# A two-layer graph network on one core: 288 counted chunks for 264, matrices of 512 and 448 columns, fewer row buffers

## The chip, the core and the metric

One core of a Trainium2 chip runs the whole program. The metric is the device time of one execution in microseconds; the figure given for a kernel is the median of its runs. The engines are named as the profile names them: PE is TensorE (PEld its weight loads), DVE is VectorE, ACT is ScalarE, POOL is GpSimd and SP is SyncE.

## What is computed

There are 6250 nodes of 256 values and 100000 edges, sorted by destination, with random sources. The destination density falls along the node numbers: edge e of E ends at about node 6250 (e/E)^2, so the early nodes have many edges each.

```
x = layernorm(x + L0(x));  x = layernorm(x + L1(x))
L0: summed = segment_sum(x[src], dst);  agg = summed / max(deg_in, 1)
    out = concat(x, agg) @ weight;  return out / norm(out) + bias
L1: h = x * rsqrt(deg_out);  m = segment_sum(h[src], dst) * rsqrt(deg_in)
    y = m @ W_gc + b_gc + x @ W_res + b_res
    y = y + top2_of_64_experts(y)          # gelu feed-forward, 256-512-256
    return batchnorm(y) * gamma + beta
```

## The kernel before

Both layers need a sum over edges, `segment_sum`. The kernel cuts the edges into NCH = 782 chunks of 128 and treats them in two ways, with the same split in both layers.

The first DCH = 264 chunks are *counted*. `counts` (L724 to L760) makes of each chunk two one-hot matrices, of its sources (`low_rows`, L705) and of source block and destination within a window of ten nodes (`oha`, L737), and multiplies them on PE (L756, 490 columns) to numbers of edges. When a group of chunks with one window ends, DVE adds the window's first column (L745) and ACT copies the other nine (L747) into an adjacency matrix kept in the on-chip memory: `adj_a` for nodes 0 to DENSE = 448 (ACH = 200 chunks), `adj_b` for nodes EDGE = 384 to EDGE + MORE = 752 (64 chunks). The matrices are later applied to all node rows by `dense_product` (L412 to L440): for each of NT = 49 node tiles of 128, six matmuls (L424) of three bf16 parts by two halves of the columns, for each matrix. A `Track` hands them out in halves of a tile, three matmuls a half. Layer 1 (the first one, L0 above) applies `adj_a` and `adj_b` one after the other, layer 2 both together. Each product is as wide as its matrix.

The other NG = 518 chunks are *gathered*: POOL issues an indirect DMA that fetches the 128 source rows (`gather_rows`, L387) into one of `nbuf` row buffers, and PE multiplies them, three bf16 parts of 256 columns, by a one-hot matrix of destinations (L664 in layer 1, L1175 in layer 2; the one-hots come from DVE four chunks at a time, `near4`, L409). Groups of chunks (GGRP) share one accumulator; at the end of a group ACT copies it (`sums`, L611 and L1179), PE transposes it (L394) and DVE adds it to `acc` (L401). Layer 1 has 9 row buffers (and for the first 64 chunks 7 others, in float32), layer 2 has 12.

One loop step is one gathered chunk, and all else is laid over these steps. `Track` spreads a list of pieces evenly between a first and a last step; `Steps` calls a piece some steps later; `staged` runs a generator in which `yield n` is a pause of n steps. PE, DVE, ACT and SP execute exactly in the order in which the loop emits (`manual_schedule`), so a piece that is late on one of these engines holds up all behind it; the same holds for DMAs on SP's queue. In layer 1:

- steps 0 to X_END = 44: the rows of x are split into three bf16 parts and stored (`three`, tiles of pool `wx3`), the matrices are cleared
- step 53 to A_END = 262: the 200 chunks of `adj_a` are counted; x times the own half of the weight (`own`, L697) is stored; `sources` counts the sources of the gathered chunks (matmuls of 49 columns, L721), until END
- A_END to END = 320: the 64 chunks of `adj_b` are counted; the dense product of `adj_a` begins and lasts to DA_END = 386
- END to DA_END: the matrices are summed to in-degrees, piece by piece of 128 nodes (`by_destination`, L785, 49 matmuls of one column at L794 for each of 7 pieces, then an add for each piece to `deg`)
- DA_END + 3 to DB_END = 476: dense product of `adj_b`
- from END + 2: every B_GAP = 3.8 steps a node tile whose sums are complete starts `first_layer` (`layer1`, L496 to L558: loads of `xw` and `xb` on SP, the product with the weight L509, norms on DVE and ACT, stores). The first ND = 6 node tiles wait for the dense products, the other 43 go first.

In layer 2 the dense products take steps 2 to D2_END = 116 (their node rows come over SP in tiles `x3`); after that `layer2` (L1043 onwards) starts a tile every T_GAP = (gathered - 128)/49 = 7.96 steps: residual (L1066) and graph product (L1070), top 2 of the experts' logits, ranks, and a table of tokens (L1203). Every 40 steps SP also issues a fill of 1792 KB with zeros. Routing, the experts' loop and the final normalization come after and share no code with the change.

`acc`, the two matrices, the constants, the one-hots and all buffers share the on-chip memory. At the start `acc` is cleared by ACT, which copies a tile `nothing` of zeros piece by piece (L269); `rel` holds each edge's place relative to its group's base, for all chunks.

Of the kernel before, what the change touches and what calls it, by code (L numbers as in the profile page):

```python
# [9 lines left out]
F32 = mybir.dt.float32  # L10
F16 = mybir.dt.float16
BF16 = mybir.dt.bfloat16
# [20 lines left out]

ACH, DCH = 200, 264
DENSE, EDGE, MORE = 448, 384, 368
ND = (EDGE + MORE + P - 1) // P
# [13 lines left out]
DX = D + NEXP  # L50
LAYER = {"xw": 3, "xb": 3, "po": 2, "o": 5, "rv": 2, "h3": 2}

# [88 lines left out]
def gnn_moe_kernel(  # L141
# [78 lines left out]
    with ExitStack() as gctx:  # L220
# [27 lines left out]

        rel = ep.tile([P, NCH], F32, name="rel")
        ngp = (NG + OHB - 1) // OHB * OHB  # L250
# [8 lines left out]
        extra = ep.tile([1, 2], I32, name="extra")  # L259
        nothing = ep1.tile([P, 512], F32, name="nothing")  # L260
        nc.vector.memset(nothing, 0.0)
# [4 lines left out]
        for h in range(2):  # L266
            for i in range(0, NACC, 512):
                n = min(512, NACC - i)
                nc.scalar.copy(acc[:, h, i : i + n], nothing[:, :n])  # L269
        with tc.tile_pool(name="pl", bufs=1) as pl, tc.tile_pool(name="pps", bufs=1, space=PSUM) as pps:  # L270
# [49 lines left out]
            bases(of_gathered)  # L320
            nc.vector.tensor_sub(rel[:, DCH:], dst_f[:, DCH:], base[:, DCH:])
            group_bases(of_gathered)
# [11 lines left out]
            nc.vector.memset(near[:, NG:], OUTSIDE)  # L334
            nc.vector.tensor_copy(near[:, :NG], rel[:, DCH:])

# [18 lines left out]
            nc.vector.tensor_scalar(out_w[:, :DCH], rel[:, :DCH], float(DWIN), None, op0=OP.is_ge)  # L355
            nc.vector.tensor_scalar(out_w[:, DCH:], rel[:, DCH:], float(P), None, op0=OP.is_ge)
            nc.vector.scalar_tensor_tensor(out_w, rel, 0.0, out_w, op0=OP.is_lt, op1=OP.add)
            real = pl.tile([P, 1], F32, name="real")
# [137 lines left out]
        def layer1(wk, ps, row, agg, rdeg, rsq_out, free, used=None):  # L496
# [24 lines left out]
            ss, sd = sm[:, 0:1], sm[:, 1:2]  # L521
            junk = wk.tile([P, D], F32, name="junk", bufs=2)
            nc.scalar.activation(junk, o, AF.Square, accum_out=ss)
# [47 lines left out]
        with ExitStack() as c:  # L571
            wk = c.enter_context(tc.tile_pool(name="wkg", bufs=2))
            ps1 = c.enter_context(tc.tile_pool(name="ps1", bufs=1, space=PSUM))
            ps2 = c.enter_context(tc.tile_pool(name="ps2", bufs=2, space=PSUM))
            nbuf, xgrp = 9, 0
            while GGRP[xgrp][0] - DCH < FIRST:
                xgrp += 1
            xch = GGRP[xgrp][0]
            bufs = []
            rsq_out = wk.tile([P, NT], F32, name="rsq_out", bufs=1)  # L580
# [124 lines left out]
            def low_rows(ohc, c0):  # L705
                ohl = ohc.tile([P, P, OHB], BF16, name="ohl")
                nc.vector.tensor_tensor(ohl, iota_lo, lo[:, None, c0 : c0 + OHB].to_broadcast([P, P, OHB]),
                                        op=OP.is_equal)
                return ohl

            def high_rows(pool, c0):
                ohh = pool.tile([P, NT, OHB], BF16, name="ohh")
                nc.vector.tensor_tensor(ohh, iota_hi, hi[:, None, c0 : c0 + OHB].to_broadcast([P, NT, OHB]),
                                        op=OP.is_equal)
                return ohh
# [8 lines left out]
            def counts(ohc, psa):  # L724
                where = {}
                for j, (c0, g) in enumerate(DGRP):
                    for ch in range(c0, c0 + g):
                        where[ch] = (j, ch == c0, ch == c0 + g - 1)
                lows, places, pa = {}, {}, [None]

                def prepare(ch):
                    if ch >= DCH:
                        return
                    if ch % OHB == 0:
                        lows[ch] = low_rows(ohc, ch), high_rows(ohc, ch)
                    oha = ohc.tile([P, NT * DWIN], BF16, name="oha", bufs=4)
                    nc.vector.tensor_scalar(oha, iota_h, rel[:, ch : ch + 1], None, op0=OP.is_equal)  # L737
                    places[ch] = oha

                def add(j, pa):  # L740

                    adj, most = (adj_a, DENSE - DWIN) if j < len(AGRP) else (adj_b, MORE - DWIN)
                    b = nc.vector.value_load(base_i[0:1, j : j + 1], min_val=0, max_val=most)
                    a = adj[:, :, ds(b, 1)]
                    nc.vector.tensor_add(a, a, pa[:, :, 0:1])  # L745
                    b = nc.scalar.value_load(base_i[0:1, j : j + 1], min_val=0, max_val=most)
                    nc.scalar.copy(adj[:, :, ds(b + 1, DWIN - 1)], pa[:, :, 1:])  # L747

                def one(ch):
                    for k in range(0, 3) if ch == 0 else (2,):  # L750
                        prepare(ch + k)
                    j, first, last = where[ch]
                    if first:
                        pa[0] = psa[0].tile([P, NT, DWIN], F32, name="pa")
                    low, high = (v[:, :, ch % OHB] for v in lows[ch - ch % OHB])
                    nc.tensor.matmul(pa[0].rearrange("p t w -> p (t w)"), low, places.pop(ch), start=first, stop=last)  # L756
                    by_source(low, high)
                    if last:
                        steps.after(2, lambda pa=pa[0]: add(j, pa))

                return [lambda ch=ch: one(ch) for ch in range(DCH)]


            def sources():
                made = {}

                def prepare(c0):
                    if c0 < NCH:
                        ohh = high_rows(ohp, c0)
                        ohs = ohp.tile([P, P, OHB], BF16, name="ohs")  # L770
                        nc.vector.tensor_tensor(ohs, iota_lo, lo[:, None, c0 : c0 + OHB].to_broadcast([P, P, OHB]),
                                                op=OP.is_equal)
                        made[c0] = ohs, ohh

                def one(c0):
                    for k in (0, 1) if c0 == DCH else (1,):
                        prepare(c0 + k * OHB)
                    ohs, ohh = made.pop(c0)
                    for k in range(min(OHB, NCH - c0)):
                        by_source(ohs[:, :, k], ohh[:, :, k])  # L780

                return [lambda c0=c0: one(c0) for c0 in range(DCH, NCH, OHB)]


            def by_destination(psg):  # L785

                pieces = [(adj_a, d, min(P, DENSE - d), d // P) for d in range(0, DENSE, P)]
                pieces += [(adj_b, d - EDGE, min(P, EDGE + MORE - d), d // P) for d in range(EDGE, EDGE + MORE, P)]
                pg = psg.tile([P, len(pieces)], F32, name="pg")

# [6 lines left out]
                def add():  # L797
                    for w, (_, _, n, t) in enumerate(pieces):
                        a = deg[:n, t : t + 1]
                        nc.vector.tensor_add(a, a, pg[:n, w : w + 1])  # L800

# [29 lines left out]

            X_END, A_END, END = 44, 262, 320
            DA_END, DB_END, B_GAP = 386, 476, 3.8
            with tc.manual_schedule(engines=ordered), ExitStack() as c1:
                cx, ca, cb, hold, cd, cg = (ExitStack() for _ in range(6))
                wx3 = cx.enter_context(tc.tile_pool(name="wx3", bufs=7))
                rows_of_g = gathered()
# [9 lines left out]
                def dense(end, adj, n, to):  # L847
                    psd = cd.enter_context(tc.tile_pool(name="psd", bufs=1, space=PSUM, side="right"))
                    xd = cd.enter_context(tc.tile_pool(name="xd", bufs=4, side="right"))

# [8 lines left out]
                def work(i):  # L859
                    nonlocal due, wl, psl, ohp, dense_done  # L860
                    if i == X_END + 9:
# [10 lines left out]
                        psa[0] = ca.enter_context(tc.tile_pool(name="psa", bufs=3, space=PSUM))  # L872
                        wx = ca.enter_context(tc.tile_pool(name="wx", bufs=3))
                        every = counts(ohc, psa)
# [20 lines left out]
                    if i == DA_END + 3:  # L895
                        dense_done = DENSE // P
                        cd.close()
# [251 lines left out]
        with ExitStack() as c:  # L1149
            st = c.enter_context(tc.tile_pool(name="st2", bufs=1))  # L1150
            ohg = c.enter_context(tc.tile_pool(name="ohg2", bufs=4))
            wk = c.enter_context(tc.tile_pool(name="wkg2", bufs=2))
            ps1 = c.enter_context(tc.tile_pool(name="ps3", bufs=1, space=PSUM))
            both_po = ps1.tile([P, 2, 2, P], F32, name="both_po")
            nbuf, ng2 = 12, NCH - DCH
            bufs = [st.tile([P, 2, 3, P], BF16, name=f"rows3{i}") for i in range(nbuf)]
# [28 lines left out]
            def parts3(t):  # L1185
                x3 = wk.tile([P, 2, 3, P], BF16, name="x3", bufs=5)
                nc.sync.dma_start(x3, h3_rows[t * P : (t + 1) * P])
                return x3
# [492 lines left out]
```

## Time and profile before

| | before |
|---|---|
| median of 3 runs | 2268.14 us (2264.69 to 2269.84) |
| the profiled execution | 2249.79 us |
| its span | 2248.0 us |
| mean granted PE clock | 0.886 |
| layer 1, first to last gather | 7.7 to 797.9 us |
| layer 2, first to last gather | 833.2 to 1596.8 us |
| DMA | 454.74 MB, mean 202 GB/s |

The profile is that of one execution. Its page gives busy time and instruction count of each engine and the costliest groups of instructions with their mean time in ns and the idle time ahead of them, with what ended it. The view of waits sums, by engine and line, what an engine stood still for, how often, and the longest one in us. In the table of windows each row is a stretch of the span. "remote" is a release that the view cannot assign to one instruction. The layers' stages in span time follow from the starts of the gathers of steps 53, 262, 320, 389 and 479 (86, 401, 495, 604 and 743 us) and of step 116 of layer 2 (1004 us).

### The profile page before, as it was taken

The page shows a single profiled execution, that of the slowest core. Times are in us where ns is not written, and L with a number is a line of the kernel's source. Part 1 is how long each engine was busy: PE and PEld are TensorE (multiplying, and loading weights), DVE is VectorE, ACT ScalarE, POOL GpSimd, SP SyncE. Part 2 cuts the span into 40 slices and gives each one's busy share as a digit, 9 for nine tenths or more (in the row PEclk, how much of TensorE's full clock was granted, in tenths as well). Part 3 has the DMA queues.
Part 4 walks back from the last instruction along what each step waited for, and adds up shares of the span by engine and source line. Part 5 has one row for each costly group of instructions (what it writes and reads, how often), then busy time and mean ns, then how long its engine had stood idle before and what let it go on. Part 6 is the DMA issues. An engine that isn't in the chain of part 4 may idle for free. (4 is left out here: it accounts for less than half of the span.)

```text
span 2248.0 us, 33489 instructions
## 1 busy us (share of the span) xinstructions
PE 1721.7 (77%) x9410; PEld 1233.8 (55%) x9410; DVE 1056.5 (47%) x4020; ACT 589.9 (26%) x1569; POOL 1248.4 (56%) x1440
## 2 busy tenths in 40 slices
PE   4677777788888638986767766666759998999697
PEld 2355555556656425654544444444438876877573
DVE  7655666675767541102434443344532233222398
ACT  7411123343444430000211211112212221222135
POOL 7766666656656626666666666666225544454100
PEclk8798898999989868997887987888869999999899
DMA  7756666557899746775666555555348988787353
GB/s 228 267 170 177 173 176 173 169 164 244 265 301 310 237 150 203 228 226 181 190 180 176 170 158 152 151 154 155 89 144 307 322 291 266 249 257 246 106 168 114
DMA packets 245283, 454.74 MB, mean 202 GB/s; under 512 B 36462, under 2 KB 166247, under 8 KB 245086
## 3 DMA queue, kind: packets, MB, share of 16 engines
q0 software_dynamic: 74880, 220.59, 33.8%
q1 hardware_dynamic: 167886, 230.37, 31.2%
q10 hardware_dynamic: 2320, 1.51, 0.2%
q8 instruction: 80, 1.31, 0.2%
q14 instruction: 117, 0.96, 0.1%
HBM read 386.64 MB, written 70.89 MB: 204 GB/s over the span
## 5 line engine op out<-in xcount | busy, mean ns | idle before, releaser
L387 POOL DMA_INDIRECT rows<-h_rows,src_i x518 | 497.7, 961 | 266.8 <-issue 111.5
L387 POOL DMA_INDIRECT rows<-x_rows,src_i x454 | 451.2, 994 | 247.1 <-issue 91.2
L1175 PE MATMUL both_po<-rows,oh 128*128 128x256 bf16 x1554 | 256.0, 302 | 148.9 <-ACT sums L1179 72.5
L1175 PEld LDWEIGHTS <-oh 128*128 128x128 bf16 x1554 | 180.4, 120 | 207.0 <-issue 171.8
L664 PE MATMUL po<-rows,oh 128*128 128x256 bf16 (+1 forms) x1362 | 241.3, 292 | 16.0 <-issue 12.8
L1444 POOL DMA_INDIRECT core<-ob,ix x100 | 101.4, 1014 | 204.0 <-DVE ob L1443 195.5
L1442 PE MATMUL po<-w2t,h 128*128 128x256 f32 x800 | 190.8, 388 | 1.1 <-ACT h L1435 0.5
L401 DVE TENSOR_TENSOR acc<-acc,pt 128x256 f32 x108 | 45.3, 419 | 294.5 <-remote 80.6
L1435 ACT ACTIVATE h<-ph,b1c 128x128 f32<-128x128 f32 (+1 forms) x288 | 94.3, 410 | 340.2 <-PE ph L1433 160.1
L664 PEld LDWEIGHTS <-oh 128*128 128x128 bf16 x1362 | 148.4, 120 | 60.6 <-issue 27.3
L1442 PEld LDWEIGHTS po<-w2t,h 128*128 128x128 f32 x800 | 151.0, 193 | 39.9 <-ACT h L1435 18.4
L409 DVE TENSOR_TENSOR oh<-iota_lo,near 128x512 bf16<-128x512 bf16 x244 | 101.6, 423 | 111.1 <-PE both_po L1175 81.8
L1443 DVE TENSOR_TENSOR ob<-po,b2b 128x256 f32<-128x256 f32 x100 | 42.4, 424 | 228.6 <-PE po L1442 207.7
L756 PE MATMUL pa<-oha,ohl 128*128 128x490 bf16 x264 | 105.7, 400 | 48.7 <-issue 24.2
L737 DVE TENSOR_SCALAR oha<-iota_h,rel 128x490 bf16<-128x490 f16 x264 | 94.1, 363 | 58.1 <-PE pa L756 23.2
L1421 PE MATMUL ph<-xt,w1t 128*128 128x256 f32 x448 | 118.8, 406 | 0.0
L1401 POOL DMA_INDIRECT xb<-xx_tok,ix x100 | 98.4, 984 | 27.0 <-issue 25.7
L1421 PEld LDWEIGHTS ph<-xt,w1t 128*128 128x128 f32 x448 | 110.4, 326 | 5.3 <-issue 2.6
L424 PE MATMUL pd<-adj_a,x 128*128 128x448 bf16 x294 | 106.1, 365 | 5.4 <-issue 5.3
L1083 DVE TENSOR_TENSOR xl<-xl,pR 128x320 f32<-128x320 f32 x49 | 23.8, 486 | 178.1 <-issue 87.5
L1066 PE MATMUL pR<-wres,t 128*128 128x320 f32 x196 | 77.1, 524 | 29.3 <-issue 18.5
L424 PE MATMUL pd<-adj_b,x 128*128 128x368 bf16 x294 | 96.6, 329 | 1.2 <-issue 0.9
(335 smaller groups left out, 3345.0 us busy)
## 6 DMA issues: line engine op xcount, KB each, us to landing
w1t<-in_L_gnn_w_dram SPq DMA_DIRECT2D x72, 512.0 KB
w2t<-in_L_gnn_w_dram SPq DMA_DIRECT2D x72, 512.0 KB
x3d<-x_rows SPq DMA_DIRECT2D x98, 192.0 KB
core<-zero SPq DMA_DIRECT2D x7, 1792.0 KB
ys<-core SPq DMA_DIRECT2D x48, 256.0 KB
h_rows<-h SPq DMA_DIRECT2D x49, 192.0 KB
x<-h_rows SPq DMA_DIRECT2D x49, 192.0 KB
x_rows<-x SPq DMA_DIRECT2D x24, 384.0 KB
```

The source lines that it names most:

```text
L387: nc.gpsimd.indirect_dma_start(out=r, out_offset=None, in_=table, in_offset=bass.IndirectOffsetOnAxis(ap=index, axis=0))
L409: nc.vector.tensor_tensor(oh, iota_lo, near[:, None, c0 : c0 + OHB].to_broadcast([P, P, OHB]), op=OP.is_equal)
L424: nc.tensor.matmul(pd[h, w], side(x3, s, h), adj[:, t, a:b], start=(t == 0 and s == 0), stop=(t == NT - 1 and s == 2))
L664: nc.tensor.matmul(po[:, :w], oh, r[:, s * D : s * D + w], start=(ch == c0 and s == 2), stop=(ch == c0 + g - 1 and s == 2))
L737: nc.vector.tensor_scalar(oha, iota_h, rel[:, ch : ch + 1], None, op0=OP.is_equal)
L756: nc.tensor.matmul(pa[0].rearrange("p t w -> p (t w)"), low, places.pop(ch), start=first, stop=last)
L1175: nc.tensor.matmul(po, oh, r[:, :, s, :], start=(ch == c0 and s == 0), stop=(ch == c0 + g - 1 and s == 2))
L1401: nc.gpsimd.indirect_dma_start(out=xb[:, h, :], out_offset=None, in_=xx_tok, in_offset=bass.IndirectOffsetOnAxis(ap=ix[:, 0, h : h + 1], a ...
L1421: nc.tensor.matmul(ph[:, hc], w1m[:, c, hc, :], xt[:, c], start=(c == 0), stop=(c == 1))
L1435: nc.scalar.activation(h1[:, hc].rearrange("p h m -> p (h m)"), pre[hc].rearrange("p h m -> p (h m)") if k == 0 else pre[hc], AF.Gelu, bia ...
L1442: nc.tensor.matmul(po, h1[:, hc, h, :], w2t[:, hc * D : (hc + 1) * D], start=(hc == 0), stop=(hc == 3))
L1444: i = nc.gpsimd.indirect_dma_start(out=core, out_offset=bass.IndirectOffsetOnAxis(ap=ix[:, 1, h : h + 1], axis=0), in_=ob[:, h, :], in_off ...
```

## The change

The counted chunks become 288 (216 for `adj_a`, 72 for `adj_b`), so 494 are gathered in each layer. `adj_a` covers nodes 0 to 512, `adj_b` nodes 448 to 896; both dense products become as wide. The counted groups go from 82 and 64 to 98 and 72, the gathered ones from 54 to 52; ND becomes 7, and T_GAP follows to 7.47. The schedule's steps move: A_END 236, END 290, DA_END 362, DB_END 464, B_GAP 3.6.

To make room for 14 KB more of matrices on each partition, buffers go: layer 1's row buffers 9 to 8, layer 2's 12 to 8, layer 2's `x3` 5 to 3, its one-hots 4 to 3, `x3d` 4 to 3, `oha` 4 to 3, `ohl`, `ohh` and `ohs` 3 to 2, `wx3` 7 to 5, `wx` 3 to 2, `junk` and `rv` 2 to 1. `rel` is cut to the chunks that are read later, with the rest in a tile `place` that lives only during the preparation; `nothing` is half as wide, so `acc` is cleared in 50 copies instead of 26. As EDGE = 448 is not a multiple of 128, `by_destination` sums 8 pieces aligned to node tiles, adds seven at once, and moves the half piece at the start of `adj_b` by 64 partitions with a small matmul before adding it.

```diff
...
-ACH, DCH = 200, 264
-DENSE, EDGE, MORE = 448, 384, 368
+ACH, DCH = 216, 288
+DENSE, EDGE, MORE = 512, 448, 448
...
-LAYER = {"xw": 3, "xb": 3, "po": 2, "o": 5, "rv": 2, "h3": 2}
+LAYER = {"xw": 3, "xb": 3, "po": 2, "o": 5, "rv": 1, "h3": 2}
...
-        rel = ep.tile([P, NCH], F32, name="rel")
+        rel = ep.tile([P, DCH + FIRST + 16], F32, name="rel")
...
-        nothing = ep1.tile([P, 512], F32, name="nothing")
+        nothing = ep1.tile([P, 256], F32, name="nothing")
...
-            for i in range(0, NACC, 512):
-                n = min(512, NACC - i)
+            for i in range(0, NACC, 256):
+                n = min(256, NACC - i)
...
-            nc.vector.tensor_sub(rel[:, DCH:], dst_f[:, DCH:], base[:, DCH:])
+            place = pl.tile([P, NG], F32, name="place")
+            nc.vector.tensor_sub(place, dst_f[:, DCH:], base[:, DCH:])
+            nc.vector.tensor_copy(rel[:, DCH:], place[:, : FIRST + 16])
...
-            nc.vector.tensor_copy(near[:, :NG], rel[:, DCH:])
+            nc.vector.tensor_copy(near[:, :NG], place)
...
-            nc.vector.tensor_scalar(out_w[:, DCH:], rel[:, DCH:], float(P), None, op0=OP.is_ge)
-            nc.vector.scalar_tensor_tensor(out_w, rel, 0.0, out_w, op0=OP.is_lt, op1=OP.add)
+            nc.vector.tensor_scalar(out_w[:, DCH:], place, float(P), None, op0=OP.is_ge)
+            for v, r in ((out_w[:, :DCH], rel[:, :DCH]), (out_w[:, DCH:], place)):
+                nc.vector.scalar_tensor_tensor(v, r, 0.0, v, op0=OP.is_lt, op1=OP.add)
...
-            junk = wk.tile([P, D], F32, name="junk", bufs=2)
+            junk = wk.tile([P, D], F32, name="junk", bufs=1)
...
-            nbuf, xgrp = 9, 0
+            nbuf, xgrp = 8, 0
...
+            assert xch <= DCH + FIRST + 16
...
-                ohl = ohc.tile([P, P, OHB], BF16, name="ohl")
+                ohl = ohc.tile([P, P, OHB], BF16, name="ohl", bufs=2)
...
-                ohh = pool.tile([P, NT, OHB], BF16, name="ohh")
+                ohh = pool.tile([P, NT, OHB], BF16, name="ohh", bufs=2)
...
-                    oha = ohc.tile([P, NT * DWIN], BF16, name="oha", bufs=4)
+                    oha = ohc.tile([P, NT * DWIN], BF16, name="oha")
...
-                        ohs = ohp.tile([P, P, OHB], BF16, name="ohs")
+                        ohs = ohp.tile([P, P, OHB], BF16, name="ohs", bufs=2)
...
-                pieces = [(adj_a, d, min(P, DENSE - d), d // P) for d in range(0, DENSE, P)]
-                pieces += [(adj_b, d - EDGE, min(P, EDGE + MORE - d), d // P) for d in range(EDGE, EDGE + MORE, P)]
-                pg = psg.tile([P, len(pieces)], F32, name="pg")
+                half = EDGE % P
+                pieces = [(adj_a, d, P, d // P) for d in range(0, DENSE, P)]
+                pieces += [(adj_b, d - EDGE, P, d // P) for d in range(EDGE + P - half, EDGE + MORE, P)]
+                pieces.append((adj_b, 0, P - half, EDGE // P))
+                pg = psg.tile([P, len(pieces) + 1], F32, name="pg")
...
-                    for w, (_, _, n, t) in enumerate(pieces):
-                        a = deg[:n, t : t + 1]
-                        nc.vector.tensor_add(a, a, pg[:n, w : w + 1])
+                    n = len(pieces) - 1
+                    nc.vector.tensor_add(deg[:, :n], deg[:, :n], pg[:, :n])
+                    shift = wl.tile([P, P], F32, name="shift", bufs=1)
+                    col = wl.tile([P, 1], F32, name="col", bufs=1)
+                    nc.vector.tensor_scalar(col, iota_p, float(half), None, op0=OP.add)
+                    nc.vector.tensor_scalar(shift, iota_row, col, None, op0=OP.is_equal)
+                    nc.vector.tensor_copy(col[: P - half], pg[: P - half, n : n + 1])
+                    nc.tensor.matmul(pg[:, n + 1 :], shift[: P - half], col[: P - half], start=True, stop=True)
+                    t = EDGE // P
+                    nc.vector.tensor_add(deg[:, t : t + 1], deg[:, t : t + 1], pg[:, n + 1 :])
...
-            X_END, A_END, END = 44, 262, 320
-            DA_END, DB_END, B_GAP = 386, 476, 3.8
+            X_END, A_END, END = 44, 236, 290
+            DA_END, DB_END, B_GAP = 362, 464, 3.6
...
-                wx3 = cx.enter_context(tc.tile_pool(name="wx3", bufs=7))
+                wx3 = cx.enter_context(tc.tile_pool(name="wx3", bufs=5))
...
-                    xd = cd.enter_context(tc.tile_pool(name="xd", bufs=4, side="right"))
+                    xd = cd.enter_context(tc.tile_pool(name="xd", bufs=3, side="right"))
...
-                        wx = ca.enter_context(tc.tile_pool(name="wx", bufs=3))
+                        wx = ca.enter_context(tc.tile_pool(name="wx", bufs=2))
...
-                        dense_done = DENSE // P
+                        dense_done = EDGE // P
...
-            ohg = c.enter_context(tc.tile_pool(name="ohg2", bufs=4))
+            ohg = c.enter_context(tc.tile_pool(name="ohg2", bufs=3))
...
-            nbuf, ng2 = 12, NCH - DCH
+            nbuf, ng2 = 8, NCH - DCH
...
-                x3 = wk.tile([P, 2, 3, P], BF16, name="x3", bufs=5)
+                x3 = wk.tile([P, 2, 3, P], BF16, name="x3", bufs=3)
```

## The prediction

> **What bounds the kernel now.** I read the page first, for which engines and lines carry the time.
>
> ```profile
> PE 1721.7 (77%) x9410; PEld 1233.8 (55%) x9410; DVE 1056.5 (47%) x4020; ACT 589.9 (26%) x1569; POOL 1248.4 (56%) x1440
> ...
> L387 POOL DMA_INDIRECT rows<-h_rows,src_i x518 | 497.7, 961 | 266.8 <-issue 111.5
> ...
> L1175 PE MATMUL both_po<-rows,oh 128*128 128x256 bf16 x1554 | 256.0, 302 | 148.9 <-ACT sums L1179 72.5
> ...
> L756 PE MATMUL pa<-oha,ohl 128*128 128x490 bf16 x264 | 105.7, 400 | 48.7 <-issue 24.2
> ...
> L424 PE MATMUL pd<-adj_a,x 128*128 128x448 bf16 x294 | 106.1, 365 | 5.4 <-issue 5.3
> ...
> L424 PE MATMUL pd<-adj_b,x 128*128 128x368 bf16 x294 | 96.6, 329 | 1.2 <-issue 0.9
> ```
>
> No engine is full. GpSimd issues one gather per loop step, 518 in each layer: 0.95 us of work and 0.30 us until the next, so 1.25 us is the least a step can take. The gathers really start every 1.528 us in layer 1 (790.2 us over 517) and every 1.477 us in layer 2 (763.5 over 517). Beyond 1.25 us a step that is 144 us in layer 1 and 117 us in layer 2. The view of waits says for what:
>
> ```profile
> POOL rows L387 <- remote: 92.8, 76, 3.2
> ...
> POOL rows L387 <- PE both_po L1175: 76.5, 86, 3.5
> ...
> PE both_po L1175 <- ACT sums L1179: 72.5, 22, 8.4
> ```
>
> GpSimd waits for TensorE to free a row buffer. TensorE rarely waits for rows in turn (22.8 us in layer 2); it executes in order and stands still for others' results, 72.5 us of it for the copies of group sums. So the pace is TensorE's work plus its standstills. Then busy times by stage, with boundaries at the loop steps where stages change (53, 262, 320, 389, 479, end of layer 1; in layer 2 the dense part, then the tiles). Columns: length, busy of PE, PEld, DVE, ACT, POOL, granted clock, DMA share, GB/s.
>
> ```profile
> 86.00:401.00 315.00, 237.97 (x1662) 173.93 (x1662) 186.00 (x701) 69.64 (x152) 209.48 (x210) 0.90 0.60 170
> 401.00:495.00 94.00, 71.82 (x535) 49.00 (x534) 66.62 (x253) 37.85 (x68) 58.42 (x58) 0.95 0.58 170
> 495.00:604.00 109.00, 94.42 (x835) 69.33 (x835) 63.20 (x242) 43.19 (x125) 66.80 (x69) 0.95 0.81 246
> 604.00:743.00 139.00, 110.76 (x713) 81.88 (x712) 94.38 (x363) 65.36 (x204) 89.05 (x91) 0.93 0.91 292
> 743.00:833.00 90.00, 45.87 (x227) 34.82 (x227) 51.70 (x196) 35.30 (x104) 37.88 (x41) 0.72 0.59 178
> 833.00:1004.00 171.00, 144.99 (x902) 95.67 (x903) 17.55 (x50) 4.56 (x14) 111.28 (x118) 0.92 0.73 224
> 1004.00:1597.00 593.00, 397.88 (x2085) 269.89 (x2084) 236.61 (x1181) 107.33 (x303) 385.88 (x402) 0.83 0.57 167
> ```
>
> The time per step is nearly flat: 315/209 = 1.507, 94/58 = 1.62, 109/69 = 1.58, 139/90 = 1.545, then 1.41, 171/116 = 1.474, 593/402 = 1.475, though TensorE's busy share runs from 67% to 87%. That is the puzzle of this case: a step costs about the same whatever lies in it.
>
> **The change, part by part.** *Gathers.* 24 chunks leave each layer: 48 x 1.25 = 60 us of GpSimd, or 24 x (1.528 + 1.477) = 72 us at the real pace. TensorE loses 72 matmuls of 256 columns a layer; in the timeline such starts lie 0.11 us apart, so -7.9 us each.
>
> *Wider matrices.* Starts of the 448-column products are 0.188 us apart in the timeline, of 368 columns 0.155, of 512 columns (L1203) 0.216. So 294 products of adj_a gain 0.027 and 294 of adj_b 0.060 - 0.027 = 0.033: 294 x 0.060 = +17.6 us, over both layers +35. *Counts.* 24 more of 0.206 us, +4.9; degree sums 392 matmuls for 343 at 0.03, +1.5. TensorE's work thus grows by about 26 us: +16 in layer 1, +9 in layer 2, while the steps fall by 4.6%.
>
> *Layer 1 by stage*, after's steps times a rate; the rate is before's plus the added TensorE work of a step at full price, since TensorE is in order and already late.
> Steps 53-236: 216 counts in 179 steps instead of 200 in 205, 0.231 more per step (x (0.206 + 0.049) = 0.059), own products 49 in fewer steps (+0.017), sources +0.009: 1.507 + 0.085, say 1.60; x 183 = 293, before 315: **-22**.
> 236-290: 72 counts in 49 steps (1.47 a step) against 64 in 53 (1.21): +0.054 and +0.02 for their histogram; dense halves of 3 products x 0.216 x 0.784 against 0.188 x 3 x 0.797: +0.057. 1.62 + 0.13 = 1.75; x 54 = 94.5: **0**. DVE and ACT take turns on adj_b here, 0.38 and 0.59 us plus handing over, about 1.2 us a count, 86 us for 72: below 94.5, but close.
> 290-365: +0.057 dense, first-layer tiles every 3.6 steps for 3.8: 1.65 x 75 = 124 against 109: **+15**.
> 365-467: one half of dense B a step against 1.14, but wider: 0.564 for 0.530, rate 1.575; x 102 = 161 against 139: **+22**.
> 467-494: 27 x 1.41 = 38 against 55: **-17**.
> Sum -2. The steps saved are almost eaten by stages that are made longer or denser.
>
> *Layer 2.* In the dense part TensorE is back to back: 3 x 0.11 and 2.53 pairs of 0.343 a step make most of the 1.474. The matrices add 294 x 0.060 there and nothing hides it: **+17**. The rest: 378 steps for 402. A tile holds some 3.5 us of TensorE work, and tiles come every 7.47 steps for 7.96, +0.029 a step: 1.504 x 378 = 568.5 against 593: **-24.5**.
>
> *Fewer buffers.* Row buffers 9 to 8 and 12 to 8. A gather's rows land within some 3 us, so with 8 buffers TensorE may stand still for 8 x 1.25 - 3 = 7 us before GpSimd falls behind for good, with 12 for 12 us; the longest standstill shown is 8.4. Trace of before: GpSimd waits beyond the least 144/518 = 0.278 us a step with 9 buffers and 117/518 = 0.226 with 12. If that difference came from buffers alone, one is worth 0.017 us a step: 494 x (1 + 4) x 0.017 = 43 us. It can be 0, when TensorE alone paces (a buffer that comes free later is then only filled later); a gain is excluded. I take a third, **+14**, because layer 1 differs from layer 2 in its work too. x3d tiles 4 to 3: in 608-752 TensorE waits 36.5 us in 15 waits for those loads, but their issue came mostly when the third-last tile was just done, so a fourth buffer was hardly used: 0 to 1 us for each wait, +15; I take **+2**. Behind that load on SyncE stand the tiles' loads and stores, so what it waits ACT and DVE wait. Layer 2's x3 5 to 3 adds a wait of the load for TensorE's third-last tile; behind it stand fills of 1792 KB: 0 to 8 us, **+3**. oha 4 to 3: DVE then waits for the count just before (23.2 us of such waits now), with the row one-hots queued behind; two counts of 1.2 us cover it: 0 to +23, **+1**. rv, junk, ohl, ohs, wx and wx3 sit in loops whose order has more steps between uses than buffers: 0 to 3 us, taken at 0. The start: 50 zero copies for 26 on ACT, +4 us, end before ACT's wait of 5.66 us at 23.2 for its first rows, which takes them; without that cover +4. The shift product and five small DVE operations replace seven adds: 0, at most 1 us either way.
>
> *A rule of the skill speaks against this.* The row: after TensorE stood still from 1424.05 to 1429.53 its clock was halved:
>
> ```profile
> 1427.80:1434.60 6.80, 5.07 (x21) 3.76 (x21) 0.76 (x2) 1.92 (x6) 4.03 (x5) 0.50 0.42 117
> 1434.60:1440.00 5.40, 4.14 (x23) 2.52 (x22) 2.57 (x16) 0.53 (x1) 3.53 (x4) 1.00 0.58 153
> ```
>
> The Trainium skill, page "TensorE: Matmul & The Clock Gate", says that an idle window of about 3.4 us brings the clock to half (part 1, "The HAM clock gate"), and advises no idle gaps above some 3 us ("Why this matters for your kernels"). Fewer buffers mean longer gaps. By the rule, if the clock of the tile stage goes from 0.83 to 0.78, its 398 us of TensorE cost 398 x 0.05/0.83 = 24 us. By the row, the stage already runs at 0.83 and keeps the same 1.475 a step as the dense part at 0.92, so most of that is slack. My +14 lies between.
>
> Sum: -2 + 17 - 24.5 + 14 + 2 + 3 + 1 = +10.5, on the profiled run 2249.8 to 2260.3. That run is 18.3 us below the median of the runs, so on the median 2268.1 + 10.5, about **2279 us**. I keep every wait of before elsewhere; routing, experts and finale (from 1640) do not change.
>
> **Rivals.**
> *The pace of a step stays as it is.* For it: the flat rates above, and over blocks of 20 steps TensorE work of 15 and of 24.5 us in layer 2 took 29.5 and 29.3 us. Added work then sinks into standstills: -72 for the steps, +17 for the full dense part: -55, **2213**. Against it: in layer 1 blocks of 12, 18.3 and 24.4 us of work took 28.1, 30 and 32.5, a slope of 0.36. With that slope for layer 1's stages, layer 2's tiles at 1.475 and half the buffer costs it is about -32, still this side. Chance 0.33 for this case, from 2205 to 2260.
> *Row buffers decide, slower.* Place: layer 2's tile stage, L1175 behind the sums. The price is all 43 us instead of 14, so +39.5, **2308**. It decides once TensorE's standstills pass 7 us often, or GpSimd's waits there pass 0.30 us a step. Speaks against it that only few now pass 7. Chance 0.22.
> *The dense part of layer 1 is bound by its loads*, at DMA share 0.91: with three x3d tiles +15, 2292, within my range. That the change does not do what it says I exclude: the counts of gathers and products follow from the constants.
>
> **How the numbers follow.** Likeliest case, 2262 to 2300: 0.45. Flat pace: 0.33. Buffers: 0.22. The likeliest's low end meets no change; "within 0.2%", 4.5 us, is about what a measurement of this kernel can tell from none, 0.10 in all. Slower: 0.22 and most of 0.45: 0.56; faster 0.34. With signs on both sides the range reaches from the middle of the flat case to the middle of the buffers case and a little on: 2220 to 2315.
>
> **What would show it.** Right: gather period 1.52 to 1.55 in layer 2's tile stage, about 1.62 in its dense part, layer 1's last gather about 796 us after the start as before. Wrong by the flat pace: periods of 1.475 to 1.50 everywhere, layer 1 over 30 us shorter. Wrong by the buffers: POOL's waits for TensorE in layer 2 well over 117 us although it gathers less, clock below 0.80 there. If 236-290 takes over 100 us, the DVE and ACT turns on adj_b have become the bound.

## The result, and the profile after

The changed kernel takes 2282.1 us (median of 11 runs, 2267.9 to 2293.27), the kernel before 2268.14 (11 runs, 2261.87 to 2277.72); the ratio is 1.0054, with a 95% interval of 1.003 to 1.0078. The forecast of 2279 is met, and the profile shows that this is luck: errors of opposite sign cancel. Here is the page of the changed kernel; in it before's L387 is L390, L1175 L1188, L756 L760, L424 L427, L737 L741, L745 L749, L747 L751, L664 L668, L721 L725.

```profile
PE 1723.3 (76%) x9258; PEld 1208.6 (53%) x9329; DVE 1082.3 (48%) x4053; ACT 605.6 (27%) x1613; POOL 1197.6 (53%) x1391
...
L390 POOL DMA_INDIRECT rows<-h_rows,src_i x494 | 474.5, 961 | 264.4 <-issue 102.6
L390 POOL DMA_INDIRECT rows<-x_rows,src_i x430 | 424.3, 987 | 327.2 <-PE po L668 147.0
...
L760 PE MATMUL pa<-oha,ohl 128*128 128x490 bf16 x288 | 114.1, 405 | 113.2 <-ACT adj_b L751 59.9
...
L741 DVE TENSOR_SCALAR oha<-iota_h,rel 128x490 bf16<-128x490 f16 x288 | 102.6, 364 | 125.9 <-PE pa L760 42.9
```

Two lines of the page before, to compare:

```profile
L387 POOL DMA_INDIRECT rows<-x_rows,src_i x454 | 451.2, 994 | 247.1 <-issue 91.2
...
L737 DVE TENSOR_SCALAR oha<-iota_h,rel 128x490 bf16<-128x490 f16 x264 | 94.1, 363 | 58.1 <-PE pa L756 23.2
```

Read the last column: TensorE now stands still 113 us ahead of the counting matmul where it was 49, and DVE 126 us ahead of `oha` where it was 58, while POOL gathers less and yet waits longer in layer 1. The table of windows, cut at the changed schedule's steps (53, 236, 290, 365, 467, end of layer 1; layer 2 to step 116, and on), says where; columns as before.

```profile
88.80:376.90 288.10, 217.22 (x1571) 160.34 (x1570) 191.11 (x713) 76.44 (x165) 184.28 (x183) 0.93 0.60 169
376.90:538.00 161.10, 97.19 (x542) 56.37 (x552) 82.20 (x277) 45.13 (x81) 51.93 (x54) 0.77 0.33 93
538.00:661.10 123.10, 105.41 (x909) 74.85 (x922) 72.73 (x278) 49.61 (x148) 72.40 (x75) 0.96 0.80 244
661.10:817.30 156.20, 121.61 (x750) 83.16 (x749) 91.35 (x343) 60.04 (x186) 100.09 (x103) 0.98 0.88 272
817.30:856.00 38.70, 24.20 (x136) 17.64 (x134) 26.62 (x100) 17.38 (x53) 25.02 (x27) 0.86 0.74 221
889.90:1064.10 174.20, 158.02 (x911) 96.79 (x930) 18.22 (x47) 4.95 (x15) 110.78 (x116) 0.96 0.73 220
1064.10:1627.80 563.70, 380.40 (x1984) 257.38 (x2008) 239.41 (x1191) 109.07 (x302) 362.81 (x378) 0.86 0.58 167
```

| steps | forecast, us | measured, us |
|---|---|---|
| layer 1, 0 to 53 | as before (77.4) | 81.1 |
| 53 to 236 | 293 | 288.1 |
| 236 to 290 | 94.5 | **161.1** |
| 290 to 365 | 124 | 123.1 |
| 365 to 467 | 161 | 156.2 |
| 467 to the end | 38 | 38.7 |
| layer 2, 0 to 116 | 191 with x3 | **174.2** |
| 116 to the end | 568.5, and 14 for buffers | **563.7** |

One stage, in which the 72 chunks of `adj_b` are counted, is 67 us over; layer 2 is 36 us under with its buffer costs. What follows layer 2's last gather took 638 us against 651. That part's code is the same in all kernels, and those of the experiments below that keep the data took 638 to 647 us for it, with no order between kernels with the change and kernels without; I take the 13 us of the profiled pair as scatter.

### The profile page after: what moved, and what is told of

Its sections match the earlier page's. It is cut to its first block, busy times and chain, and to the rows that moved or that the text cites. A ratio compares the mean times of both kernels' runs of the same rounds, so it can differ in the third digit from the quotient of the medians.

```text
span 2266.2 us, 33440 instructions
## 1 busy us (share of the span) xinstructions
PE 1723.3 (76%) x9258; PEld 1208.6 (53%) x9329; DVE 1082.3 (48%) x4053; ACT 605.6 (27%) x1613; POOL 1197.6 (53%) x1391
## 5 line engine op out<-in xcount | busy, mean ns | idle before, releaser
L390 POOL DMA_INDIRECT rows<-h_rows,src_i x494 | 474.5, 961 | 264.4 <-issue 102.6
L390 POOL DMA_INDIRECT rows<-x_rows,src_i x430 | 424.3, 987 | 327.2 <-PE po L668 147.0
L1188 PE MATMUL both_po<-rows,oh 128*128 128x256 bf16 x1482 | 243.5, 298 | 121.1 <-ACT sums L1192 57.8
L1188 PEld LDWEIGHTS <-oh 128*128 128x128 bf16 x1482 | 170.8, 119 | 182.7 <-issue 139.9
L668 PE MATMUL po<-rows,oh 128*128 128x256 bf16 (+1 forms) x1290 | 227.9, 291 | 3.1 <-issue 2.7
L760 PE MATMUL pa<-oha,ohl 128*128 128x490 bf16 x288 | 114.1, 405 | 113.2 <-ACT adj_b L751 59.9
L668 PEld LDWEIGHTS <-oh 128*128 128x128 bf16 x1290 | 140.1, 120 | 53.0 <-issue 16.2
L741 DVE TENSOR_SCALAR oha<-iota_h,rel 128x490 bf16<-128x490 f16 x288 | 102.6, 364 | 125.9 <-PE pa L760 42.9
L427 PE MATMUL pd<-adj_a,x 128*128 128x512 bf16 x275 | 105.0, 382 | 3.0 <-issue 3.0
L427 PE MATMUL pd<-adj_b,x 128*128 128x448 bf16 x294 | 104.5, 355 | 3.4 <-DMA x<-h_rows 1.6
L1192 ACT COPY sums<-both_po 128x256 f32<-128x256 f32 x52 | 19.3, 371 | 303.3 <-PE both_po L1188 179.4
L725 PEld LDWEIGHTS <-ohl 128*128 128x128 bf16 x288 | 33.7, 117 | 121.5 <-issue 118.8
```

The lines of the kernel that those rows point to most:

```text
L390: nc.gpsimd.indirect_dma_start(out=r, out_offset=None, in_=table, in_offset=bass.IndirectOffsetOnAxis(ap=index, axis=0))
L427: nc.tensor.matmul(pd[h, w], side(x3, s, h), adj[:, t, a:b], start=(t == 0 and s == 0), stop=(t == NT - 1 and s == 2))
L668: nc.tensor.matmul(po[:, :w], oh, r[:, s * D : s * D + w], start=(ch == c0 and s == 2), stop=(ch == c0 + g - 1 and s == 2))
L1188: nc.tensor.matmul(po, oh, r[:, :, s, :], start=(ch == c0 and s == 0), stop=(ch == c0 + g - 1 and s == 2))
```

## The experiments

The comparisons of one group ran on one chip each; before took 2251.27 us in the first group, 2262.79 in the second, 2248.33 in the third and 2044.58 in the last. Between groups, totals are compared only as ratios. Stage times come from one profile each, and the same code scatters: layer 2's dense part took 171.2 to 176.6 us in the kernels with the change that leave its work as it is, its tile steps 1.468 to 1.495 us.

**1. Is it the oha buffers or the number of counts?** Theory 1, a closed loop, comes from the order in which the engines execute. In that stage it stands like this (c, d, e, f, g are counts in a row; PE has two accumulators `pa`):

```
DVE:  one-hot f | one-hot g | ohh, ohs | add c | one-hot h | ...
PE:   count c | count d | count e (takes c's accumulator) | ...
```

With three `oha` buffers one-hot g takes d's place and waits until PE has counted d. The add of c stands behind it in DVE's queue. ACT can copy c only after the add, and PE can count e only when ACT has freed c's accumulator. So each link waits for the next. The changed kernel's timeline shows one turn:

```profile
463.66 0.37 PE L760 MATMUL pa<-oha,ohl 128*128 128x490 bf16 x1
...
464.07 0.35 DVE L741 TENSOR_SCALAR oha<-iota_h,rel 128x490 bf16<-128x490 f16 x1 [0.38 <-PE ph L725]
...
464.34 0.25 DVE L717 TENSOR_TENSOR ohh<-iota_hi,hi 128x196 bf16<-128x196 bf16 x1
464.51 0.41 DVE L775 TENSOR_TENSOR ohs<-iota_lo,lo 128x512 bf16<-128x512 bf16 x1
464.86 0.37 DVE L749 TENSOR_TENSOR adj_b<-adj_b,pa 128x49 f32 x1
465.32 0.53 ACT L751 CAST adj_b<-pa 128x441 f32 x1 [2.02 <-DVE adj_b L749]
465.90 0.37 PE L760 MATMUL pa<-oha,ohl 128*128 128x490 bf16 x1 [1.82 <-ACT adj_b L751]
...
466.31 0.35 DVE L741 TENSOR_SCALAR oha<-iota_h,rel 128x490 bf16<-128x490 f16 x1 [1.07 <-PE pa L760]
```

Count, one-hot (its wait is put down to L725, PE's product right behind the count), add, copy, count: 2.24 us from 463.66 to 465.90, one link after the other, and 161.1/72 = 2.24 us a count is the mean of the stage. The rival is that DVE and ACT, in turns on `adj_b`, cannot do 1.47 counts a step whatever the buffers.

```diff
-                    oha = ohc.tile([P, NT * DWIN], BF16, name="oha")
+                    oha = ohc.tile([P, NT * DWIN], BF16, name="oha", bufs=4)
```

> The changed kernel with one edit: oha has 4 buffers again. Theory 1 (a closed loop): with three oha buffers DVE builds the one-hot of count k+3 only when TensorE has done count k, and the adds into adj_b stand behind it in DVE's queue; TensorE in turn needs the accumulator that ACT frees after that add. With a fourth buffer the loop opens: steps 236 to 290 fall from 161 us to 95 to 110, the kernel to about 2225 to 2235, ratio to before 0.98 to 0.987. Theory 2 (too many counts for the taking of turns of DVE and ACT on adj_b): the stage stays at 150 to 165 us, the kernel at about 2282.

Measured: 2209.74 us, ratio 0.9813 (0.9786 to 0.984); the stage falls from 161.1 to 111.7 us. That is a little above the expected 95 to 110; the ratio lies in the expected 0.98 to 0.987 (the kernel before is faster on this chip too). Theory 1 holds; the rival explains at most what is left, 1.55 us a count.

The mirror of it, the kernel before with `bufs=3`:

> The kernel before with one edit: oha has 3 buffers instead of 4. Theory 1: at 1.21 counts a step the loop closes only in the steps that hold two counts; steps 262 to 320 go from 95 us to 105 to 140, the kernel to about 2278 to 2310. Theory 2: nothing changes, 95 us and 2268. Steps 53 to 262 (0.98 counts a step, three accumulators): at most 10 us longer under theory 1.

Measured: ratio 1.0099 (1.0062 to 1.0136), steps 262 to 320 go from 94.8 to 119.5 us, steps 53 to 262 from 315.3 to 319.7. The loop closes here too, and costs less, 25 us, at 1.21 counts a step. These are the waits of the counting stage in the changed kernel, then with a fourth buffer (us in total, times, longest):

```profile
ACT adj_b L751 <- DVE adj_b L749: 88.3, 51, 4.3
...
PE pa L760 <- ACT adj_b L751: 56.3, 36, 2.7
...
DVE oha L741 <- PE pa L760: 22.9, 29, 1.3
```

```profile
ACT adj_b L751 <- DVE adj_b L749: 43.2, 38, 4.9
...
PE pa L760 <- ACT adj_b L751: 27.6, 29, 2.1
```

The wait of `oha` for the count is itself small, 22.9 us, and 1.1 us with the fourth buffer; what it cost shows one and two engines further on.

Density instead of the buffer, oha still 3:

```diff
-            X_END, A_END, END = 44, 236, 290
+            X_END, A_END, END = 44, 236, 304
```

> The changed kernel with END 304 for 290: the 72 counts of adj_b are spread over 63 steps instead of 49 (1.14 a step), oha stays at 3; the first layer's tiles start 14 steps later, their other due times stay. Theory 1: fewer steps hold two counts, steps 236 to 304 take 115 to 135 us, against 161 + 14 x 1.64 = 184 in the changed kernel; the kernel at about 2230 to 2255. Theory 2 (each count costs some 2.2 us by taking turns): still 72 x 2.2 = 158 us or more for the stage, so 158 to 184, the kernel 2260 to 2282.

Measured: ratio 0.9844 (0.9809 to 0.9878); steps 236 to 304 take 133.9 us, 1.86 a count. So a count has no fixed price, as the rival would have it, and the loop costs most where many steps hold two counts: spread, the same 72 counts with the same three buffers cost 53 us less than 161.1 and the changed kernel's next 14 steps (25.7).

The loop cut at its other link, the place of the add, oha still 3:

```diff
-                        steps.after(2, lambda pa=pa[0]: add(j, pa))
+                        steps.after(1, lambda pa=pa[0]: add(j, pa))
```

> The changed kernel, oha still with 3 buffers, but the add of a count into its matrix is emitted one step after the count instead of two, so it stands in DVE's queue ahead of the one-hots of later counts. Theory 1 (the loop is closed by the add's place behind one-hots that wait for TensorE): steps 236 to 290 fall from 161 us to 95 to 120, total near 2220 to 2235 on a chip where before takes 2251. Rival (three oha buffers cost by themselves, whatever stands behind): the stage stays above 140 us.

Measured: ratio 0.9771 (0.9746 to 0.9797); the stage takes 102.0 us, less than with four buffers and the old order. In this stage three buffers cost nothing by themselves; it is what stands behind their wait. The edit moves the adds into `adj_a` too, and steps 53 to 236 took 295.9 us for 288.1; whether from the order there or from scatter was not tried.

**2. Do the row buffers cost?** Before, with `nbuf` 8 in both layers, layer 2's one-hots 3 and `x3` 3.

> The kernel before with the changed kernel's row buffers: 8 in layer 1 for 9, 8 in layer 2 for 12, there also x3 with 3 for 5 and the one-hots with 3 for 4. The prediction put +14 on the row buffers and +3 on x3: layer 2's tile steps from 1.478 to about 1.51, 2268 to about 2285. Rival (row buffers decide): +43, 2311. Rival (TensorE alone paces): within 4 us of 2268, and GpSimd's waits only change what they are put down to.

Measured: ratio 0.9974 (0.996 to 0.9988), layer 2's tile steps 1.470 us against 1.478, its dense steps 1.483 against 1.472. Fewer row buffers cost nothing in the whole; the ratio is even slightly below 1, which the stages do not explain (in the profiles layer 1 is 6.6 us longer than in the kernel before, profiled in another group, and the gain lies behind layer 2).

**3. Does width cost in layer 2?** The changed kernel with oha 4, layer 2's products on `adj[:, t, 0:448]` and `[:, t, 0:368]`, which leaves out the columns beyond.

> The changed kernel with 4 oha buffers; layer 2's dense products are as narrow as before, 448 and 368 columns (the last 64 and 80 columns of the matrices are left out). The prediction put +17 us on the width there. If it is right, the dense part falls from 176.6 us to about 160 and the kernel by 17. If the width fills TensorE's slack first (1.363 us of work in a step of 1.474 before), the part falls only to 116 x 1.474 = 171, and the kernel by about 5.

Measured: ratio 0.9805 (0.978 to 0.9831), the dense part 178.0 us against 176.6 with the full width, where oha 4 alone has 0.9813. On the same chip, the full width took 174.6 and 176.0 us in two other kernels. A price of 17 us is excluded; one of a few us would be lost in the scatter.

**4. What sets layer 2's step?** One matmul a chunk instead of three:

```diff
-                        for s in range(3):
-                            nc.tensor.matmul(po, oh, r[:, :, s, :], start=(ch == c0 and s == 0),
-                                             stop=(ch == c0 + g - 1 and s == 2))
+                        nc.tensor.matmul(po, oh, r[:, :, 0, :], start=(ch == c0), stop=(ch == c0 + g - 1))
```

> The changed kernel with 4 oha buffers; in layer 2 each gathered chunk gets one matmul instead of three (two of the three bf16 parts of its rows are left out; they are still fetched). It asks what sets layer 2's step. Theory of the prediction (TensorE's work and standstills pace, added work at full price): 0.22 us less work a step, so the tile steps fall from 1.468 us to about 1.25 to 1.30 and the dense ones from 1.52 to 1.30. Rival (something in the gathers or in the order of other engines sets about 1.47): dense and tile steps stay above 1.42.

Measured: 1.467 us a dense step, 1.465 a tile step. With all three matmuls, on the same chip, two kernels took 1.505 and 1.517 in the dense part and 1.492 each in the tile part. So 0.03 to 0.05 us of the 0.22 come back. In this kernel's window of the tile part TensorE is busy 60% of the time, at a clock of 0.75, where the changed kernel's is at 67% and 0.86, and the gathers do not hurry:

```profile
1010.00:1560.00 550.00, 328.55 (x1228) 186.04 (x1248) 239.63 (x1187) 108.46 (x300) 363.11 (x376) 0.75 0.59 171
```

The prediction's premise falls: TensorE's work does not set layer 2's step at anything like its full price. Next, the bytes:

```diff
+        h3s = h3_rows.rearrange("n h s c -> (n h s c)").rearrange("(m k) -> m k", k=D)
...
-                        gather_rows(r.rearrange("p h s c -> p (h s c)"), h3v, src_i[:, ch : ch + 1])
+                        gather_rows(r.rearrange("p h s c -> p (h s c)")[:, :256], h3s, src_i[:, ch : ch + 1])
```

> The changed kernel with 4 oha buffers; layer 2's gathers fetch 512 bytes for each of the 128 rows instead of 1536, from other rows than the reference's (the remaining columns are zeros). TensorE's work and its waits are the same. If the bytes of a gather set the step of 1.47 us, it falls to 1.25 to 1.35; if not, it stays at 1.42 to 1.50.

Measured in layer 2: 1.465 and 1.469 us a step. A third of the bytes changes nothing. (The whole, 2433.54 us, says nothing: with other data the experts' loop has other work; so too in the next run.) Last, gathers that nobody reads:

> The changed kernel with 4 oha buffers; in layer 2 TensorE multiplies a constant tile instead of the gathered rows, which are fetched (into 7 buffers) and read by nobody. A gather then waits for no product. If the release of row buffers by TensorE's products sets layer 2's step, the step falls from 1.47 to 1.25 to 1.30 us wherever TensorE leaves room (in the tile part at least); if the gathers themselves or their DMA set it, it stays at 1.42 to 1.50.

Measured in layer 2: 1.254 us a step in the first 116, so without a release to wait for GpSimd runs there at its least; 1.377 after, where many of its instructions take 1.10 us instead of 0.95. But this run cannot be read as the expectation meant it, since TensorE hardly moved meanwhile:

```profile
1253.06 0.37 PE L1190 MATMUL both_po<-still,oh 128*128 128x256 bf16 x1 [2.43 <-issue]
1253.36 1.10 POOL L390 DMA_INDIRECT rows<-h_rows,src_i  x1 [0.30 <-issue]
1254.46 0.11 PEld L1190 LDWEIGHTS <-oh 128*128 128x128 bf16 x1 [2.69 <-issue]
1254.76 1.10 POOL L390 DMA_INDIRECT rows<-h_rows,src_i  x1 [0.30 <-issue]
1255.86 0.37 PE L1190 MATMUL both_po<-still,oh 128*128 128x256 bf16 x1 [2.43 <-issue]
```

For long stretches PE starts one instruction per gather, each exactly when the gather instruction before it ends (1253.36 + 1.10 = 1254.46), and catches up only after the last gather.

So what is the 1.47 us? The traces hold one more answer: it is a mean and no pace. In the tile part of the kernel before, 327 of the 401 distances from the start of one gather to the start of the next are under 1.4 us, close to GpSimd's least; 54 over 2 us hold 82 of the 91 us beyond 1.25 us a step. The changed kernel and those of the first three groups (but the one whose gathers nobody reads) have 36 to 55 such distances, with 8 row buffers or 12, a third of the bytes (47) or one matmul (36). On the last group's chip there is none. One of them, in the kernel before, is the standstill from 1424.05 to 1429.53 that the prediction shows:

```profile
1423.56 0.49 PE L1175 MATMUL both_po<-rows,oh 128*128 128x256 bf16 x3
...
1425.26 0.96 POOL L387 DMA_INDIRECT rows<-h_rows,src_i  x1 [0.30 <-issue]
...
1426.53 0.95 POOL L387 DMA_INDIRECT rows<-h_rows,src_i  x1 [0.30 <-issue]
...
1429.11 0.37 ACT L1179 COPY sums<-both_po 128x256 f32<-128x256 f32 x1 [6.41 <-remote]
1429.29 0.95 POOL L387 DMA_INDIRECT rows<-h_rows,src_i  x1 [1.82 <-remote]
1429.53 0.80 PE L1175 MATMUL both_po<-rows,oh 128*128 128x256 bf16 x3 [5.48 <-ACT sums L1179]
```

TensorE's last product has ended at 1424.05, and ACT is idle; yet ACT's copy starts only at 1429.11, and then ACT, POOL and PE go on within 0.42 us. The copy itself takes 0.37 us. So "PE waits for ACT's sums" names the link that came last and not the cause: ACT was let go late as well. These are waits of TensorE in the tile part, in the kernel before (1004 to 1597 us) and then in the kernel profiled on the last group's chip (888 to 1396 us):

```profile
PE both_po L1175 <- ACT sums L1179: 69.2, 20, 8.4
```

```profile
PE both_po L1175 <- DMA rows<-h_rows,src_i: 103.1, 116, 3.6
PE both_po L1175 <- ACT sums L1179: 11.3, 24, 0.5
```

There, the copies come 0.5 us late at most, and TensorE waits for its rows. What holds several engines up at once on the other chips is not shown.

**5. The best version, and how much of it is order.** oha 4, the adds into `adj_b` one step earlier, END 297. A first try with oha 4 and END 304 alone:

> The changed kernel with 4 oha buffers and END 304: 72 counts over 63 steps. With oha 4 alone steps 236 to 304 took about 134 us (111.7 to step 290 and 14 x 1.59), 1.55 us a count in the count steps. If the remaining excess is the density of counts, 236 to 304 falls to 68 x 1.62 = 110, and the kernel by some 20 us to about 2190. If each count costs 1.5 us by DVE's and ACT's turns, 72 x 1.5 = 108 us also fits in 68 steps, which gives the same. If the later start of the first layer's tiles costs something, they end later and up to 10 us come back at the end of layer 1.

Measured: ratio 0.9747 (0.9711 to 0.9784); steps 236 to 304 take 117.4 us against 133.8, 16 us less, but layer 1's later stages and layer 2 took 13 us more in the profiled pair, and the two ran on different chips, so its advantage over oha 4 alone is not settled.

> The changed kernel with 4 oha buffers, the adds into adj_b one step earlier in the order, and END 297. By the loop theory steps 236 to 297 take 61 x 1.60 = 98 us against 111.7 + 7 x 1.57 = 123 with oha 4 alone; layer 2 as before it. Total 15 to 25 us below that kernel, ratio to before 0.970 to 0.976; if the later start of the first layer's tiles gives it back, as with END 304, 0.978 to 0.982.

Measured: 2172.3 us, ratio 0.9665 (0.964 to 0.969), more than expected: steps 236 to 297 take 98.0 us (1.607 a step) as forecast, and steps 53 to 236 281.4 against 288.8, which nothing in the edit explains (END 304 gave 289.1 there, and the two kernels of experiment 4 on the same chip 287.2 and 288.5). It beats both kernels. And the same order in the kernel before, with nothing else:

> The kernel before, with the adds into adj_b one step earlier in the order and nothing else (4 oha buffers, 264 counted chunks). It asks how much of the best version's gain comes from that order alone. If the loop is open in the kernel before (1.635 us a step in steps 262 to 320 against 1.58 in the stage after), 0 to 5 us: 0.998 to 1.0. If the order itself were worth what it seems in the best version, the stage would fall below 85 us and the ratio to 0.99 or less.

Measured: ratio 0.996 (0.9943 to 0.9978). So the order alone is worth some 0.4% there, a little more than expected. That chip is the one without the long distances, and in layer 1 too its steps are shorter (1.353 us in steps 262 to 320); how much of the best version's 3.35% on its own chip is order is therefore not settled.

## Why the prediction came out right

*The rates of layer 1* hold where no loop closed: 288.1 for 293, 123.1 for 124, 156.2 for 161, 38.7 for 38. Where 0.085 us a step of added TensorE work was worked out, in steps 53 to 236, the rate went from 1.507 to 1.574, by 0.067; in the first group it is about 1.53 without the change and 1.58 with it, 0.05. That fits a price of over half, but no run takes work out of layer 1, so that TensorE's work is the reason is not shown there.

*Steps 236 to 290 failed.* Two terms were mis-sized. "oha 4 to 3 ... two counts of 1.2 us cover it: 0 to +23, +1" was worth 49 us (161.1 to 111.7). I looked at when the buffer comes free, and named what stands behind the wait (one-hots), but did not follow that the add behind it releases the accumulator which TensorE needs for the count that frees the buffer. And with the buffer back the stage still takes 17 us more than 94.5, 1.55 us a count instead of "about 1.2"; with the earlier add it takes 7.5 more, 1.42 a count. What part of that is the turns of DVE and ACT, the runs do not separate. The warning sign that the prediction ends with, over 100 us in this stage, was the right one, but its cause was put to DVE's and ACT's turns.

*Layer 2 failed the other way.* "Nothing hides it: +17" for the wider products was +3.4 in the changed kernel's profile, and taking the width away again gained nothing that the scatter lets one see. "Back to back" was a misreading: the line shown has TensorE busy for 144.99 of 171 us, and the products counted up there make 1.20 of 1.474 us a step. The tile steps cost 1.495, not 1.504 and 0.037 for buffers. The row buffers, +14, are worth nothing in the experiment; the rival that put them at 43 falls with it, and the rule on idle gaps of the Trainium skill ("TensorE: Matmul & The Clock Gate", "Why this matters for your kernels": no idle gaps above some 3 us) did not come to bear, for the clock of the tile part went from 0.83 to 0.86. The first step that failed is the premise "the pace is TensorE's work plus its standstills". It rests on standstills put down to ACT's copies, and in the one shown above the copy was itself let go late. The flat rates were seen and called the puzzle, and then a rate was priced as if they were not there. In layer 2 the flat-pace rival had the right numbers, 1.502 and 1.495 us; as a pace of each step it is wrong too, for the mean is made of many steps near 1.25 us and few long ones.

*The signs* named for being right all failed: 1.495 us in the tile part for 1.52 to 1.55, 1.502 in the dense part for about 1.62, layer 1's last gather at 856.0 us for about 796.

*The start* took 81.1 us for 77.4; in the other kernels with the change it is about 80, in those without 77 to 78.5. So part of the price named "without that cover", +4, is paid; what of the change causes it was not tried.

Measured against the forecast by stage: the counting stage +67, layer 2 -36 with its buffers, the start +4, layer 1's other stages -10, small terms that no stage shows -3, between the layers -1, the end -13. That is +8: the profiled pair differs by 18 us where 10.5 were forecast.

What makes the long distances, and with them layer 2's 1.47 us, stays open. It is not the bytes, not the number of row buffers, and hardly TensorE's work or the products' width. The last group's chip says that the program alone does not fix it: there the kernel with the earlier add, nearly the kernel before, gathers every 1.279 us in the dense part and every 1.268 in the tile part.

## What to carry to other kernels

When a buffer is taken from a pool, follow its new wait round: what stands behind the waiting instruction on its engine, who needs that, and whether the chain comes back to whoever frees the buffer. If it does, the price is the whole chain once a turn and not the wait in the list, and it shows on other engines. When the time per step is the same in stages with very different work, look at how the single steps are spread before you call their mean a pace, and do not price added work at full before an experiment that takes work away has shown that it counts. Where a wait names an engine, look whether that engine was idle too. A total that comes out right proves nothing of its terms; compare stage by stage.

## What had not been expected of the hardware

Beside gathers that wait for nothing TensorE started one instruction per gather, some 1.40 us each, for some 240 us on end; in the kernels whose gathers wait for row buffers TensorE's starts lie 0.11 to 0.22 us apart beside running gathers. By what way the gathers do this, if it is they, no run shows. And chips differ: the kernel before took 2248 to 2263 us in the first three groups and 2044.58 in the last, where the one kernel profiled has gather steps near the 1.25 us that GpSimd needs in layer 2.
